# A graph attention layer on one core: the spread of the attention vectors and the order of the first group

## The chip, the cores and the metric

The kernel runs on one core of one Trainium2 chip. The metric is the time on the device in microseconds, from the first to the last instruction of the core; times of a kernel are the median of several executions. The kernel before took 2331.45 us (three executions, 2331.03 to 2332.3). Times inside the kernel are counted from the start of its span.

The engines are called TensorE (PE in the profile; its weight loads are PEld), VectorE (DVE), ScalarE (ACT), GpSimd (POOL) and SyncE (SP, which only issues transfers). Each works through its own queue in order and waits for the others by semaphores.

## The reference

`x` is 128 graphs of 64 nodes with 512 features, all fp32. Cut to what matters:

```python
h = relu(layernorm(x))                               # (128, 64, 512)
# layer 1: H = 4 heads, W_heads (4, 512, 512), a_heads (4, 1024)
Wh = einsum('bnf,hfo->bhno', h, W_heads)
f1 = einsum('bhno,ho->bhn', Wh, a_heads[:, :512])
f2 = einsum('bhno,ho->bhn', Wh, a_heads[:, 512:])
e  = f1[..., :, None] + f2[..., None, :]
e  = where(e > 0, e, 0.01 * e)
e  = where(adj > 0, e, -1e9)                         # one adj (64, 64) for all graphs
h1 = elu(softmax(e) @ Wh)                            # heads side by side: (128, 64, 2048)
# layer 2: the same with one head, W_out (2048, 512), a_out (1024)
out = elu(gat(h1, adj, W_out, a_out))
y   = relu(out @ w1 + b1) @ w2 + b2 + out            # w1, w2 (512, 512)
result = x + layernorm(y) * gamma + beta
```

## The kernel before

The 8192 rows are 64 tiles of 128 rows (two graphs each), and 16 groups of four tiles. The matrix products of most of the work are done by a fast scheme with 7 block products in place of 8. It needs sums of blocks of each weight matrix ("weight sums"), which GpSimd computes once, in the first group, and stores to DRAM (`tc`), from where they are loaded like weights. The first group (g = 0) is different from the others: it computes `h W` head by head with plain products (`head_w`), so that TensorE has work before the sums are there.

The scores need `W a` for each head. The two halves of `a` of head m are spread over 128 partitions by a product with a column of the identity (`spread_a`), and VectorE multiplies them with the rows of W and adds up (`fold`) into `wa`. `project_f` then multiplies `wa` with the transposed h.

```python
X[0] = load(0)
ar = wk.tile([2 * H, O], FP, tag="elu", name="ar", bufs=3)
nc.sync.dma_start(out=ar, in_=a_heads.rearrange("h (r p) -> (h r) p", p=O))
# ... cut: the other tiles of the group, adj, masks

mats = [W_heads[h] for h in range(H)]                          # matrices 0 to 3
mats += [W_out[h * O:(h + 1) * O, :] for h in range(H)]        # 4 to 7
mats += [w1, w2]                                               # M1 = 8, M2 = 9
homes = ("h11", "h22", "h12", "wh2", "out", "hS", "out", "hS", "out", "out")

def spread_a(m):
    ab = []
    for c in range(2):
        pb = flat(bank(f"pab{m}_{c}"))
        r = 2 * m + c
        nc.tensor.matmul(
            pb, ident[0:2 * H, r:r + 1].to_broadcast([2 * H, P]), ar, start=True, stop=True
        )
        ab.append(pb)
    return ab

def weight_sums(m, after=None):       # four tensor_tensor on GpSimd, then two stores to TC[m]
    ...

def norm1(t):
    # ... cut: bn_stats, bn_aggr, + eps on VectorE
    # rstd (pow) and nb = -mean * rstd on GpSimd
    LAST["nb"] = nc.gpsimd.tensor_scalar(nb, mean, rstd, -1.0, ALU.mult, ALU.mult)
    HN[t] = big.tile([P, F], FP, tag="hn", name=f"hn{t}", bufs=G)
    nc.scalar.activation(HN[t], X.pop(t), AF.Relu, bias=nb, scale=rstd)

def transpose_h(t):                   # 4 transposes on TensorE, a copy on ScalarE (pth, hT)
    ...

def project_f(g):
    # ... cut: 16 small products into pf
    L = sm.tile([P, 2, P], FP, tag="L", name=f"L{g}", bufs=1)
    for q in range(2):
        nc.scalar.activation(L[:, q], pf, AF.Identity, bias=isq[:, q, 1:2], scale=isq[:, q, 0:1])
    U = sm.tile([P, P], FP, tag="U", name=f"U{g}", bufs=1)
    nc.vector.tensor_scalar(U, pf, isf[:, 1:2], isf[:, 0:1], ALU.mult, ALU.add)
    R = sm.tile([P, H, P], FP, tag="R", name=f"R{g}", bufs=1)
    eng = nc.vector if g == 0 else nc.gpsimd
    eng.tensor_tensor(R, U[:, None, :].to_broadcast([P, H, P]),
                      headrow[:, :, None].to_broadcast([P, H, P]), ALU.mult)

def head_w(m, j):                     # h W of head m, tile j: four products, a copy on ScalarE
    pb = aux([P, O], f"hw{m}_{j}")
    for k in range(KC):
        LAST["pe"] = LAST["hw", m, j] = nc.tensor.matmul(
            pb, HT[j][:, k, :], MT[m][:, k, :], start=k == 0, stop=k == KC - 1)
    nc.scalar.copy(flat(HW[j][:, m]), pb)
```

`scores1` makes the scores of a group (s1pe), `attn_weights(p)` the softmax of two tiles (a chain of eight instructions on VectorE and one on ScalarE, ending in s1A), `transpose_weights(p)` turns them (s1pt, at). `attend0(h, r)` multiplies the weights with h W (pu) and applies elu, `turn0(h, r)` transposes the result (ptu) into h11, h12, hS, h22. `project2` is the product with W_out (g_b), `project1` of the groups from 1 on is the product with W_heads (g_a). The softmax of the second layer has the names s2.

The first group before, in the order in which it is written down (a scheduler moves some of it by its priorities):

```python
for t in range(G):
    norm1(t)
for t in range(G, 2 * G):
    prefetch(t)
norms, scores, turns = stage_a(1)
ab = [spread_a(m) for m in range(3)]
for m in range(3):
    fold(m, ab[m])
for j in range(G):
    transpose_h(j)
    head_w(0, j)
weight_sums(0, LAST["nb"])
fold(3, spread_a(3))
masks()
weight_sums(1, LAST["nb"])
for j in range(3):
    head_w(1, j)
more_sums(4)                # fetch and weight_sums
project_f(0)
weight_sums(2, LAST["nb"])
head_w(1, 3)
more_sums(5)
head_w(2, 0)
scores1(0)
attn_weights(0)
attn_weights(1)
weight_sums(3, LAST["nb"])
norms[0]()                  # norms of tiles 4 and 5
norms[1]()                  # 6 and 7
more_sums(6)
new_h1(0)
for j in range(1, G):
    head_w(2, j)
more_sums(7)
transpose_weights(0)
head_w(3, 0)
attend0(0, 0)
attend0(1, 0)
head_w(3, 1)
# ... cut: attends and turns of the four heads, the rest of head_w(3)
for g in range(NG):
    # ... cut
    if g == 0:              # project2(0) with this beside it, the sums of w1 and w2 last
        mixed = side1 + attn[:2] + norms[:1] + attn[2:] + norms[1:] + [nothing] * 3
        run(project2(g), mixed + early + scores + turns + [
            load_rows, lambda: sums_late(M1), lambda: sums_late(M2)
        ])
```

Of the kernel before, what the change touches and what calls it, by code (L numbers as in the profile page):

```python
# [22 lines left out]
def gat_preln_kernel(  # L23
# [87 lines left out]
    ar = wk.tile([2 * H, O], FP, tag="elu", name="ar", bufs=3)  # L111
    nc.sync.dma_start(out=ar, in_=a_heads.rearrange("h (r p) -> (h r) p", p=O))
# [11 lines left out]
    isq = const.tile([P, 2, 2], FP, name="isq")  # L124
    wa = const.tile([P, KC, 32], FP, name="wa")

    def masks():
# [8 lines left out]
        nc.vector.tensor_reduce(isf, id32[:, 0:2 * H].rearrange("p (c h) -> p c h", c=2), AX.X, ALU.add)  # L136
        for q in range(2):
# [17 lines left out]
    homes = ("h11", "h22", "h12", "wh2", "out", "hS", "out", "hS", "out", "out")  # L155
    MT, TC = {}, {}

    def fetch(m, after=None):
# [3 lines left out]
        if after is not None:  # L162
            behind(ins, after, "not in front of what is needed first")

    def spread_a(m):

        ab = []
        for c in range(2):
            pb = flat(bank(f"pab{m}_{c}"))
            r = 2 * m + c  # L170
            nc.tensor.matmul(
                pb, ident[0:2 * H, r:r + 1].to_broadcast([2 * H, P]), ar, start=True, stop=True
            )
            ab.append(pb)
# [12 lines left out]
    def weight_sums(m, after=None):  # L187
# [11 lines left out]
        nc.gpsimd.tensor_tensor(s[1][:, 1], b21, s[0][:, 1], ALU.subtract)  # L199
        TC[m] = [dram.tile([P, 2, 2, Q], FP, name=f"tc{m}_{i}") for i in range(2)]  # L200
        for i in range(2):
            nc.gpsimd.dma_start(out=TC[m][i], in_=s[i])

# [111 lines left out]
    def norm_stats(src, tag, t):  # L315
# [4 lines left out]
        if tag == "n1" and t >= G:  # L320
            behind(ins, LAST["pe"], "x may come late: not in front of what is urgent")
# [10 lines left out]
    def norm1(t):  # L332
# [6 lines left out]
        nc.scalar.activation(HN[t], X.pop(t), AF.Relu, bias=nb, scale=rstd)  # L339
# [8 lines left out]
    def transpose_h(t):  # L348
        pt = aux([P, KC, P], f"pth{t}")
        for k in range(KC):  # L350
            nc.tensor.transpose(pt[:, k, :], HN[t][:, ts(k, P)], ident)
        HT[t] = wk.tile([P, KC, P], FP, tag="hT", name=f"hT{t}", bufs=4)
        nc.scalar.copy(HT[t], pt)

    def project_f(g):
# [12 lines left out]
        for q in range(2):  # L368
            nc.scalar.activation(L[:, q], pf, AF.Identity, bias=isq[:, q, 1:2], scale=isq[:, q, 0:1])
        U = sm.tile([P, P], FP, tag="U", name=f"U{g}", bufs=1)  # L370
        nc.vector.tensor_scalar(U, pf, isf[:, 1:2], isf[:, 0:1], ALU.mult, ALU.add)
        R = sm.tile([P, H, P], FP, tag="R", name=f"R{g}", bufs=1)
        eng = nc.vector if g == 0 else nc.gpsimd
        eng.tensor_tensor(
            R, U[:, None, :].to_broadcast([P, H, P]), headrow[:, :, None].to_broadcast([P, H, P]),
            ALU.mult,
        )
# [460 lines left out]
    for t in range(G):  # L838
# [5 lines left out]
    ab = [spread_a(m) for m in range(3)]  # L844
    for m in range(3):
        fold(m, ab[m])
    for j in range(G):
        transpose_h(j)
        head_w(0, j)
# [142 lines left out]
```

## Time and profile before

| engine | busy us | instructions |
|---|---|---|
| TensorE, products | 2289.5 | 11856 |
| TensorE, weight loads | 1896.2 | 11856 |
| VectorE | 1274.2 | 2227 |
| ScalarE | 901.9 | 1621 |
| GpSimd | 1014.9 | 908 |

The span of the profiled execution is 2329.7 us. The mean granted clock of TensorE over it was 0.995 of full speed.

The page of a profile has the busy time of each engine, then the span in 40 equal slices in which a digit is the busy share of a slice in tenths. Other views of the same trace are the timeline (each line: start, duration, engine, line of the kernel, operation, output<-input, sizes, count, and in brackets the idle time before it and what ended it), and the list of waits (who waited for what: total, times, longest).

A busy TensorE in this trace is not always a fast one: the duration of one pass has to be looked at beside the share. In the first group the page cannot show much, since a slice of it is 58 us long; the timeline from 0 to 230 us is the view that the change is read from.

### The profile page before, as it was taken

To read this page: it belongs to the slowest core of one execution; us is meant where nothing else is said; L and a number is where in the kernel's file an instruction comes from. 1 tells how busy PE (TensorE), PEld (TensorE's weight loads), DVE (VectorE), ACT (ScalarE), POOL (GpSimd) and SP (SyncE) were. 2 spreads that over 40 slices of the span, in tenths; PEclk is the share of its full clock that TensorE was granted. 3 is DMA by queue.
4 is the path that set the end of the run, shared out by engine and by line. 5 is a ranking of instruction groups with operands and counts; after the bars stand their busy time and mean duration, and the time that the engine had idled before them with its cause. 6 is when DMAs were issued, how large, how long until landed. Compare 5 with 4: busy or idle time off the path is not lost. (4 is left out here: it accounts for less than half of the span.)

```text
span 2329.7 us, 33260 instructions
## 1 busy us (share of the span) xinstructions
PE 2289.5 (98%) x11856; PEld 1896.2 (81%) x11856; DVE 1274.2 (55%) x2227; ACT 901.9 (39%) x1621; POOL 1014.9 (44%) x908
## 2 busy tenths in 40 slices
PE   8899999999999999999999999999999999999997
PEld 3477888888888888888888888888888888888885
DVE  4645464554656555464654655556465554644527
ACT  2523525244252533525244252533525344251512
POOL 6554443525444253443524444263443535433334
PEclk9999999999999999999999999999999999999999
DMA  7435454454545545454454645445454454635543
GB/s 271 163 109 176 132 181 131 147 175 132 183 134 159 158 136 181 135 177 131 146 180 128 185 136 159 156 136 183 132 171 137 146 180 132 181 122 161 165 149 104
DMA packets 255011, 361.14 MB, mean 155 GB/s; under 512 B 23768, under 2 KB 143608, under 8 KB 254848
## 3 DMA queue, kind: packets, MB, share of 16 engines
q1 hardware_dynamic: 249744, 341.16, 47.1%
q0 software_dynamic: 4576, 16.81, 2.0%
q8 instruction: 96, 1.57, 0.3%
q10 hardware_dynamic: 528, 1.05, 0.1%
q14 instruction: 67, 0.55, 0.1%
HBM read 331.66 MB, written 27.26 MB: 154 GB/s over the span
## 5 line engine op out<-in xcount | busy, mean ns | idle before, releaser
L297 PE MATMUL g_b<-w,h 128*128 128x256 f32 x2560 | 593.1, 379 | 0.0
L297 PEld LDWEIGHTS g_b<-w,h 128*128 128x128 f32 x2560 | 481.1, 190 | 64.7 <-issue 2.1
L282 PE MATMUL g_a<-z,w 128*128 128x256 f32 x1440 | 342.8, 381 | 0.0
L282 PE MATMUL g_a<-zs_z,w 128*128 128x256 f32 x1440 | 338.0, 383 | 4.0 <-ACT t_a L248 4.0
L282 PEld LDWEIGHTS g_a<-zs_z,w 128*128 128x128 f32 x1440 | 271.0, 191 | 64.0 <-issue 24.3
L282 PEld LDWEIGHTS g_a<-z,w 128*128 128x128 f32 x1440 | 273.3, 191 | 41.8 <-DVE g_a L586 4.9
L297 PE MATMUL g_b<-w,hS 128*128 128x256 f32 x1024 | 239.3, 380 | 0.0
L590 POOL TENSOR_TENSOR hS<-hS,h 128x512 f32<-128x512 f32 x60 | 77.9, 1299 | 354.3 <-DVE hS L556 354.3
L297 PEld LDWEIGHTS g_b<-w,hS 128*128 128x128 f32 x1024 | 192.7, 191 | 25.1 <-issue 0.2
L554 ACT ACTIVATE exc<-g_a 128x512 f32<-128x512 f32 x240 | 142.7, 594 | 163.4 <-DVE g_a L586 95.6
L556 DVE SCALAR_TENSOR_TENSOR h<-exc,g_a 128x512 f32<-128x512 f32 x180 | 123.6, 686 | 141.9 <-ACT exc L555 141.3
L555 ACT ACTIVATE exc<-exc 128x512 f32<-128x512 f32 x240 | 151.4, 631 | 6.7
L671 POOL TENSOR_TENSOR h<-h,h 128x512 f32<-128x512 f32 x64 | 86.9, 1366 | 132.9 <-PE g_b L297 132.9
L671 POOL TENSOR_TENSOR h<-hS,h 128x512 f32<-128x512 f32 x64 | 81.3, 1272 | 144.0 <-PE g_b L297 144.0
L472 ACT COPY at<-s1pt 128x512 f32<-128x512 f32 x64 | 34.6, 590 | 280.7 <-PE s1pt L468 280.7
L307 POOL TENSOR_TENSOR zs_z<-zS,z 128x512 f32<-128x512 f32 x60 | 84.6, 1410 | 130.6 <-PE g_a L282 121.2
L813 POOL TENSOR_TENSOR xr<-xr,bs 128x512 f32<-128x512 f32 x64 | 94.3, 1477 | 73.3 <-DMA xr<-in_x_dram 39.7
L297 PE MATMUL g_d<-w,rt 128*128 128x256 f32 x512 | 121.8, 380 | 2.1 <-DVE o L805 1.0
L282 PE MATMUL g_c<-ot,w 128*128 128x256 f32 x512 | 122.8, 383 | 0.6 <-DVE ot L775 0.6
L695 DVE SCALAR_TENSOR_TENSOR jf<-wh,ao 128x512 f32<-128x512 f32 x128 | 98.0, 801 | 33.0 <-ACT wh L677 32.9
L282 PE MATMUL g_a<-zS,w 128*128 128x256 f32 x480 | 113.4, 379 | 0.0
L297 PEld LDWEIGHTS g_d<-w,rt 128*128 128x128 f32 x512 | 96.9, 190 | 17.2 <-DVE o L805 2.3
(162 smaller groups left out, 3538.6 us busy)
## 6 DMA issues: line engine op xcount, KB each, us to landing
w<-tc SPq DMA_DIRECT2D x624, 256.0 KB, 2.7
w<-in_L_gnn_W_out_dram SPq DMA_DIRECT2D x192, 256.0 KB, 2.7
w<-in_L_gnn_W_heads_dram SPq DMA_DIRECT2D x180, 256.0 KB, 3.1
w<-in_L_gnn_w_dram SPq DMA_DIRECT2D x96, 256.0 KB, 2.7
x<-in_x_dram SPq DMA_DIRECT2D x64, 256.0 KB, 4.1
xr<-in_x_dram SPq DMA_DIRECT2D x128, 128.0 KB, 2.6
out_dram<-o SPq DMA_DIRECT2D x128, 128.0 KB, 2.4
tc<-pt POOLq DMA_DIRECT2D x20, 512.0 KB, 3.8
```

The lines of the kernel that those rows point to most:

```text
L282: LAST["pe"] = nc.tensor.matmul(bk[:, o, :], w[:, k, ts(o, P)], a[:, k, :], start=start and o == 0 and k == 0, stop=k == 1, skip_group_che ...
L297: LAST["pe"] = nc.tensor.matmul(bk[:, j, :], a[:, k, ts(j, P)], w[:, k, :], start=start and k == 0 and j == 0, stop=i == len(ms) - 1 and k ...
L307: eng.tensor_tensor(s2, s1, a11, ALU.subtract)
L472: nc.scalar.copy(AT[t].rearrange("p b h n -> p (b h) n"), pt)
L554: nc.scalar.activation(ex, src, AF.Relu, scale=-1.0)
L555: nc.scalar.activation(ex, ex, AF.Exp, scale=-1.0)
L556: nc.vector.scalar_tensor_tensor(dst, ex, -1.0, src, ALU.add, ALU.max)
L590: nc.gpsimd.tensor_tensor(dst, dst, H1["22"][:, h], ALU.add)
L671: nc.gpsimd.tensor_tensor(dst[:, h], x0[:, h], x1[:, h], ALU.subtract)
L695: nc.vector.scalar_tensor_tensor(junk, WH2[g][:, j], 1.0, ao[:, c, :], ALU.mult, ALU.mult, accum_out=f[:, c, j:j + 1],)
L813: nc.gpsimd.tensor_tensor(xr, xr, bs, ALU.add)
```

## The change

The change is to the first group alone. It has these parts:

- The spread of `a` uses all 128 rows of the array: `ar` is a full tile whose other rows are set to zero, and the column of the identity has 128 rows. The spreads of heads 1 to 3 come one by one between the transposes and the `h W` of head 0, with explicit dependencies that keep them in place, where six of the eight products stood at the start before.
- The factor R of groups 0 and 1 is made by four instructions on ScalarE straight from the projection (with `hsf`, two more small instructions of the masks), in place of U and R on VectorE or GpSimd.
- The norms of tiles 4 to 7 depend on the last fold (VectorE) and on an `h W` (ScalarE), and the sums of matrix 2 stand before them on GpSimd and the sums of matrix 3 behind them.
- The fetches and sums of matrices 4 to 7 have a fixed order, matrix 6 goes to another buffer, and the sums of w1 and w2 are moved from the end of the first `project2` into the `h W` of head 3 and the beginning of `project2`.
- Attends and turns of head h are put one after the other between the `h W` of heads 2 and 3, with the transposes of the next group's tiles among them; those of the last heads go beside the first products of `project2`.

```diff
-    ar = wk.tile([2 * H, O], FP, tag="elu", name="ar", bufs=3)
-    nc.sync.dma_start(out=ar, in_=a_heads.rearrange("h (r p) -> (h r) p", p=O))
+    ar = wk.tile([P, O], FP, tag="elu", name="ar", bufs=3)
+    nc.vector.memset(ar, 0.0)
+    nc.sync.dma_start(out=ar[0:2 * H], in_=a_heads.rearrange("h (r p) -> (h r) p", p=O))
...
-    homes = ("h11", "h22", "h12", "wh2", "out", "hS", "out", "hS", "out", "out")
+    homes = ("h11", "h22", "h12", "wh2", "out", "hS", "h22", "out", "out", "out")
...
-            nc.tensor.matmul(
-                pb, ident[0:2 * H, r:r + 1].to_broadcast([2 * H, P]), ar, start=True, stop=True
-            )
+            ins = nc.tensor.matmul(pb, ident[:, r:r + 1].to_broadcast([P, P]), ar, start=True, stop=True)
+            if after is not None:
+                behind(ins, after, "not in front of it")
...
         if tag == "n1" and t >= G:
-            behind(ins, LAST["pe"], "x may come late: not in front of what is urgent")
+            behind(ins, LAST["pe" if t >= 2 * G else "fold"], "not in front of what is urgent")
...
-        nc.scalar.activation(HN[t], X.pop(t), AF.Relu, bias=nb, scale=rstd)
+        ins = nc.scalar.activation(HN[t], X.pop(t), AF.Relu, bias=nb, scale=rstd)
+        if t == 1:
+            behind(ins, LAST["hT"], "the first product waits for it")
+        if G <= t < 2 * G:
+            behind(ins, LAST["pe"], "not in front of what is urgent")
...
+        if g < 2:
+            for h in range(H):
+                nc.scalar.activation(
+                    R[:, h], pf, AF.Identity, bias=hsf[:, 0, h:h + 1], scale=hsf[:, 1, h:h + 1]
+                )
...
-    ab = [spread_a(m) for m in range(3)]
-    for m in range(3):
-        fold(m, ab[m])
-    for j in range(G):
-        transpose_h(j)
-        head_w(0, j)
+    fold(0, ab)                          # ab = spread_a(0), ahead of transpose_h(0)
+    fold(1, spread_a(1, LAST["th"]))
     weight_sums(0, LAST["nb"])
-    fold(3, spread_a(3))
+    head_w(0, 0)
+    transpose_h(1)
+    fold(2, spread_a(2, LAST["pe"]))
+    head_w(0, 1)
+    transpose_h(2)
+    fold(3, spread_a(3, LAST["pe"]))
+    weight_sums(1, LAST["nb"])
+    weight_sums(2, LAST["nb"])
+    head_w(0, 2)
+    transpose_h(3)
+    head_w(0, 3)
     masks()
...
+    head_w(1, 0)
     project_f(0)
+    head_w(1, 1)
+    norms[0]()
+    norms[1]()
+    weight_sums(3, LAST["nb"])
+    sums_of(4, LAST["hw", 0, 0])         # fetch and weight_sums
     scores1(0)
     attn_weights(0)
     attn_weights(1)
+    head_w(1, 2)
+    head_w(1, 3)
+    fetch(5, LAST["hw", 0, 2])
+    fetch(6, LAST["hw", 1, 3])
+    ahead = fetch(7, LAST["hw", 1, 3])
+    ahead = weight_sums(5, ahead)
+    head_w(2, 0)
+    ahead = weight_sums(6, ahead)
+    head_w(2, 1)
+    transpose_weights(0)
+    weight_sums(7, ahead)
+    new_h1(0)
+    head_w(2, 2)
+    transpose_weights(1)
+    attend0(0, 0)
+    head_w(2, 3)
+    attend0(1, 0)
+    turn0(0, 0)
     head_w(3, 0)
+    attend0(2, 0)
+    turn0(1, 0)
+    transpose_h(4)
     head_w(3, 1)
...
+    head_w(3, 3)
+    sums_of(M1, LAST["hw", 3, 0])
     attend0(1, 1)
+    turn0(3, 0)
+    transpose_h(7)
+    side1 = [
+        lambda: (attend0(2, 1), turn0(1, 1)), lambda: (attend0(3, 1), turn0(2, 1), project_f(1)),
+        lambda: turn0(3, 1), lambda: (scores1(1), attn_weights(2)), nothing, lambda: attn_weights(3),
+        lambda: (fetch(M2, LAST["hw", 3, 3]), weight_sums(M2, LAST["pe"])), nothing,
+    ] + turns[1:] + [nothing] * 2
...
-            run(project2(g), mixed + early + scores + turns + [
-                load_rows, lambda: sums_late(M1), lambda: sums_late(M2)
-            ])
+            run(project2(g), mixed + early + scores + turns + [load_rows])
```

## The prediction

> **What bounds the kernel now.** I read the page's busy shares first:
>
> ```profile
> PE 2289.5 (98%) x11856; PEld 1896.2 (81%) x11856; DVE 1274.2 (55%) x2227; ACT 901.9 (39%) x1621; POOL 1014.9 (44%) x908
> ...
> PEld 3477888888888888888888888888888888888885
> ```
>
> TensorE is busy for 98% of the span. The second line is its weight loads in 40 slices of 58 us: 8 tenths everywhere except in the first four slices (3, 4, 7, 7) and the last. So what is left to gain lies in the first 230 us, the first group, which is the part that the change rewrites. The waits of TensorE, for all 2329.7 us, say the same:
>
> ```profile
> PE hw L612 <- ACT hw L615: 7.5, 1, 7.5
> PE pab L171 <- POOL n1rs L327: 5.4, 1, 5.4
> PE g_a L282 <- ACT t_a L248: 4.0, 1, 4.0
> PE pth L351 <- ACT hT L353: 3.2, 2, 2.6
> PE s1pt L468 <- DVE s1A L426: 2.6, 2, 2.1
> ```
>
> All five waits fall before 215 us. A busy TensorE can also be a slow one, so the timeline of TensorE comes next (start, duration, what, count of passes; the four products of an h W are eight passes):
>
> ```profile
> 5.36 10.57 PE L171 MATMUL pab<-ar,ident 8*128 8x512 f32 x12 [5.36 <-POOL n1rs L327]
> 15.87 1.11 PE L351 MATMUL pth<-ident,hn 128*128 128x128 f32 x4
> 16.91 2.07 PE L171 MATMUL pab<-ar,ident 8*128 8x512 f32 x2
> 18.91 5.46 PE L612 MATMUL hw<-pw,hT 128*128 128x512 f32 x8
> ...
> 25.78 3.70 PE L612 MATMUL hw<-pw,hT 128*128 128x512 f32 x8
> ...
> 58.54 7.13 PE L612 MATMUL hw<-pw,hT 128*128 128x512 f32 x16
> 73.21 5.61 PE L612 MATMUL hw<-pw,hT 128*128 128x512 f32 x8 [7.53 <-ACT hw L615]
> ...
> 214.72 3.78 PE L282 MATMUL g_a<-zs_z,w 128*128 128x256 f32 x8 [4.05 <-ACT t_a L248]
> ```
>
> Three losses are to be seen. (1) The spreads of eight rows take 10.57/12 = 0.88 us a pass, and the first h W takes 5.46 us where the next one takes 3.70: half speed from 5.36 to about 22.5 us, though TensorE never stops. (2) It stands still for 7.53 us at 65.7, and starts again slowly (5.61). (3) It stands still for 4.05 us at 210.7, with 3.78 for 1.89 after it.
>
> Behind (2) stand ScalarE and GpSimd. ScalarE's queue is in order, and the norm of the next group stands in it ahead of the eviction of an h W; its factor comes from GpSimd, which is in the weight sums until 66.2:
>
> ```profile
> 57.62 0.59 ACT L615 COPY hw<-hw 128x512 f32<-128x512 f32 x1 [2.85 <-PE hw L612]
> 68.81 1.52 ACT L339 ACTIVATE hn<-x,n1nb,n1rs 128x512 f32<-128x512 f32 x2 [10.60 <-POOL n1nb L337]
> ```
>
> Behind (3) stands one VectorE instruction. In the first group it takes 5.48 us, in the second 0.42:
>
> ```profile
> 207.96 5.48 DVE L418 SCALAR_TENSOR_TENSOR s2e<-s2e 128x256 f32<-128x256 f32 x1
> ...
> 354.50 0.42 DVE L418 SCALAR_TENSOR_TENSOR s2e<-s2e 128x256 f32<-128x256 f32 x1
> ```
>
> GpSimd worked without a gap from 202.08 to 214.57 meanwhile: the weight sums of w2, then the sums of z that had queued behind them.
>
> **What the Trainium skill says.** "TensorE: Matmul & The Clock Gate", Part 1, What's actually happening: the array idles at half clock, and some 3.4 us of sustained work release it. The trace agrees in part: from the first h W at 18.91 the weight loads shorten from 0.33 to 0.19 us at 22.49, after 3.6 us. But 10.57 us of work on eight rows did not release it; the page doesn't say that the count of rows matters, so I take that from the trace. "SBUF — State Buffer", Who interferes with whom: a VectorE instruction with two SBUF inputs contends with a GpSimd instruction that reads SBUF, and one fully blocks. The 5.48 against 0.42 us agrees; the folds (one input in PSUM) agree too, at 0.68 us each beside GpSimd at work.
>
> **The change, part by part.** I replay the new order of TensorE with the steps of the trace. Start to start: an h W 3.43 us (its evictions at 39.25, 42.68, 46.12 and 49.55 us), a spread pair 1.72 warm and 3.42 cold, four transposes of h 0.53, a projection 1.0, a score step 1.02, a pair of transposed weights 0.9, an attend or a turn of head 0 to 3 1.0.
>
> Start. The memset of the full `ar` stands ahead of its load. A 128x128 memset took 0.17 us, four times the width should stay under 0.5; the load's issue moves from 1.17 to about 1.3 us. TensorE starts at about 5.45.
>
> Spread and h W of head 0. 5.45 + 3.42 (first pair, cold) + 1.0 (transposes) = 9.9; by then 4.4 us of full-row work have passed, so the clock is up: + 1.72 + 3.43 = 15.1 for the first h W. Then 0.53 + 1.72 + 3.43 twice gives 26.4. The spread also covers the copy of the transposed h, which cost 0.73 us each at 29.9 and 34.8. The last tile has no spread: 0.5 + 0.75 wait + 3.43 = 31.1. VectorE's folds take 32 x 0.61 us from 10.65, as before, to 30.1, and are in nobody's way.
>
> To the first product of the second layer. h W of head 1 tile 0 (34.5), projection (35.5), tile 1 (39.0), scores (40.0; the factors L and R now come from ScalarE, 2 x 0.4 + 4 x 0.4 us, ready at about 38.1 in place of a 2.94 us R on VectorE), two more h W (46.8), two of head 2 (53.7), weights (54.6), h W (58.0), weights (58.9), attend and h W (63.4), attend and turn (65.4). Then four rounds: h W 3.43 + attend 1.0 + turn 1.0 + transposes 0.5 = 5.9 each, so 89.0. What still has to be done and was done before the first g_b in the old order: two attends, three turns, one projection, 6.0 us. That makes 95.0, against 115.1 in the trace: 20.1 us less. By cause: about 6.6 the clock, 0.7 a wait, 9.4 the stall at 65.7 (7.53 + 1.9 slow), the remaining 3.4 small waits of 101 to 110 us, where attends and turns of one head followed too closely.
>
> The stall must not come back. The sums of matrix 2 now stand before the norms of tiles 4 to 7: GpSimd ends the sums of 0 and 1 at 24.5 as before, and matrix 2 (4 x 1.23 + 1.1 + two issues of a fetch 1.6) at 32 to 36, as its buffers' stores land. The factors take some 4.3 us more, ready at 37 to 41. ScalarE does the four h (4 x 0.76) behind the h W that ends at 39.0, by 42.2 to 43.5; the next eviction that TensorE depends on is wanted at 46.8. So 3 us of slack.
>
> Stall at 210. The sums of w1 and w2 move from there into the h W of head 3 and the first products of the second layer. The stretch from the first g_a to the transposed weights of the second softmax (s2pt) takes 224.54 - 189.35 = 35.19 us in the first group and 364.92 - 336.86 = 28.06 in the second. Without those sums the first should equal the second: 7.1 us less.
>
> What it adds. Those sums now lie beside the softmax of tiles 4 to 7, whose three-step chain on VectorE has two SBUF inputs in three of eight instructions. In the old order two of these were stretched by 1.1 and 0.7 us and TensorE waited 2.1. I put 2.5 us on more of it. The wait at 159.6 (2.6 us and 1.9 slow; a norm behind six sums of z on GpSimd) keeps its order and stays.
>
> Sum: 20.1 + 7.1 - 2.5 = 24.7 us less. All later groups have the same order on TensorE, VectorE, ScalarE and GpSimd. 2331.45 - 24.7 = 2306.8.
>
> **The rivals.** First: the full-row spread doesn't raise the clock, since 120 of its rows are zeros and the array may count arithmetic, not rows. For it: only eight-row spreads were seen. Then the second pair, its neighbours and half of the first h W stay slow, and the gain shrinks by some 3.5 us: 2310. Second: a new wait takes the place of the old one. TensorE now changes between h W, attend, turn and transposes every microsecond, with ScalarE in order between them; a round gives ScalarE 3.6 us and VectorE 2.7 us of work in 5.9, so it fits, but one late link costs each of four rounds. And GpSimd is, by this replay, nearly without a pause from 12 to 117 us in the new order; if the softmax of tiles 4 to 7 is blocked as L418 was, 5 us come back, and a stop of over 3 us costs 2 more at half clock: 2313 to 2316. Third: the gain is larger, because attends, turns and first g_b interleaved cover the softmax that cost 2.1 us, and the wait at 159.6 goes too: 2300. Fourth: only the first group gains nothing because weights arrive late. Against it: the DMA engines are full until 30 us in both, and TensorE never waited for a weight there.
>
> **Range and chances.** The centre is 2307. A second stall costs up to 10 us, the third rival gives 7: low 2299, high 2318. The gain that would be over 2%, 46.6 us, exceeds all idle and slow time that I find in the first 230 us (about 24 us of waits with the 5.4 of the start, and some 15 at half speed), and nothing in the order could cost 46. So nearly all lies within 2%.
>
> **What will show it.** Passes of the second spread pair at 0.43 us and not 0.88; the first h W at 3.7 us, ending near 15; no wait of TensorE for the eviction of h W; the first attend near 59 and the last turn near 98; L418 of the first group at about 0.4 us; g_a to s2pt in about 28 us. If the wait for s1A grows above 3 us, or a wait for a turn's or attend's copy shows up in each round, the second rival holds. If the end of the first group is early by 20 us but the total is not, a later group has changed, and I am wrong about that.

## The result, and the profile after

The changed kernel takes 2320.09 us (median of four executions, 2317.49 to 2322.69), the kernel before, measured with it, 2331.53 us. The ratio is 0.9951 [0.9933, 0.9968]: a gain of 11 us, under half of the 24.7 predicted, and 2 us outside the range. The profiled executions have spans of 2318.7 and 2329.7 us, the same 11.0 us apart, so the two traces can be compared piece by piece.

The page already shows that one slice went the wrong way (busy us, share and instructions; then the weight loads in 40 slices of 58 us):

```profile
PE 2279.3 (98%) x11856; PEld 1893.2 (82%) x11856; DVE 1288.4 (56%) x2227; ACT 903.3 (39%) x1629; POOL 1017.0 (44%) x907
...
PEld 4568888888888888888888888888888888888885
```

TensorE is busy for 10 us less, and the first two slices went from 3 and 4 to 4 and 5. But the third fell from 7 to 6 (its granted clock from 0.97 to 0.87), which no step of the prediction foresaw. VectorE's busy time grew by 14.2 us with the same count of instructions. The list of TensorE's waits names the place (total, times, longest):

```profile
PE s1pt L485 <- DVE s1A L443: 14.3, 2, 14.1
PE pab L177 <- DMA ar<-in_L_gnn_a_heads_dram: 6.6, 1, 6.6
PE pth L362 <- ACT hT L364: 2.4, 1, 2.4
```

The waits for the eviction of an h W (7.5) and for t_a (4.0) are gone. The wait for s1A, the last step of the softmax of tiles 4 and 5, has grown from 2.6 to 14.3 us.

The timeline of TensorE (start, duration, output<-input, count of passes, and in brackets the wait ahead), at the start, around that wait, and from there to the second softmax:

```profile
6.58 3.75 PE L177 MATMUL pab<-ar,ident 128*128 128x512 f32 x4 [6.58 <-DMA ar<-in_L_gnn_a_heads_dram]
10.12 1.06 PE L362 MATMUL pth<-ident,hn 128*128 128x128 f32 x4
10.97 2.30 PE L177 MATMUL pab<-ar,ident 128*128 128x512 f32 x4
13.11 3.60 PE L629 MATMUL hw<-pw,hT 128*128 128x512 f32 x8
...
100.82 1.04 PE L662 MATMUL ptu<-ident,nat 128*128 128x128 f32 x8
...
106.37 3.62 PE L304 MATMUL g_b<-w,hS 128*128 128x256 f32 x16
124.06 1.94 PE L485 MATMUL s1pt<-ident,s1A 128*128 128x128 f32 x8 [14.08 <-DVE s1A L443]
...
184.20 1.46 PE L289 MATMUL g_a<-z,w 128*128 128x256 f32 x6
...
213.62 0.60 PE L740 MATMUL s2pt<-ident,s2A 128*128 128x128 f32 x4
```

The clock is up within the second spread pair, and the first h W runs at full speed. At 110 us TensorE stops for 14.08 us, then starts at half clock (1.94 us, where the other half of these transposes takes 1.04).

On VectorE it is one instruction, the leak of the scores (L435, `max(0.01 e, e)`), with both inputs in SBUF. For tiles 0 and 1 it takes 0.69 us, for tiles 4 and 5 it takes 14.76:

```profile
42.61 0.69 DVE L435 SCALAR_TENSOR_TENSOR s1e<-s1e 128x512 f32<-128x512 f32 x1
...
105.36 14.76 DVE L435 SCALAR_TENSOR_TENSOR s1e<-s1e 128x512 f32<-128x512 f32 x1
120.16 0.69 DVE L436 TENSOR_REDUCE s1mx<-s1e 128x8 f32<-128x512 f32 x1
```

And on GpSimd, at the beginning and the end of that stretch (L672 and L688 are sums for the first product of the second layer, L205 a sum of w2, L208 its stores):

```profile
103.66 1.28 POOL L688 TENSOR_TENSOR h<-hS,h 128x512 f32<-128x512 f32 x1
104.89 2.50 POOL L672 TENSOR_TENSOR hS<-hS,h 128x512 f32<-128x512 f32 x2
...
118.32 1.25 POOL L205 TENSOR_TENSOR pt<-pw,pt 128x512 f32<-128x512 f32 x1
119.53 1.10 POOL L208 DMA_DIRECT2D tc<-pt  x2
```

From 103.66 to 119.57 us GpSimd runs thirteen sums of 1.25 us, each starting 0.03 to 0.06 us before the one in front ends. The leak ends 0.55 us after the last of them, a little less than its normal 0.69 us.

**The account.** The changed kernel has as much done 98.2 us after the start as the old one after 115.1 (the last turn, from 100.82, is through at 101.7; less two g_b of 1.73 that were already done by then): 16.9 gained. The stretch from the first g_a to the transposed weights of the second softmax is 213.62 - 184.20 = 29.42 us, of which 1.26 is a pair of s1 transposes that lay elsewhere before, so 28.16 where it was 35.19: 7.0 gained. 16.9 + 7.0 = 23.9, and 11.0 came out, so some 12.9 us are lost between. The waits for s1A grew by 11.7, and slow products follow the long one, so the stop accounts for the loss within about a microsecond.

### The profile page after: what moved, and what is told of

Same layout as the page of the kernel before. It is cut to its first block, busy times and chain, and to the rows that moved or that the text cites. A ratio compares the mean times of both kernels' runs of the same rounds, so it can differ in the third digit from the quotient of the medians.

```text
span 2318.7 us, 33251 instructions
## 1 busy us (share of the span) xinstructions
PE 2279.3 (98%) x11856; PEld 1893.2 (82%) x11856; DVE 1288.4 (56%) x2227; ACT 903.3 (39%) x1629; POOL 1017.0 (44%) x907
## 5 line engine op out<-in xcount | busy, mean ns | idle before, releaser
L688 POOL TENSOR_TENSOR h<-h,h 128x512 f32<-128x512 f32 x64 | 86.8, 1364 | 135.1 <-PE g_b L304 135.1
L688 POOL TENSOR_TENSOR h<-hS,h 128x512 f32<-128x512 f32 x64 | 81.1, 1268 | 142.6 <-PE g_b L304 142.6
```

What stands on the lines that cost most here:

```text
L688: nc.gpsimd.tensor_tensor(dst[:, h], x0[:, h], x1[:, h], ALU.subtract)
```

## The experiments

The texts on record call the theories by letters. **A**: the leak and its like are held by GpSimd's reads of SBUF, and let go when GpSimd stops; this is what the second rival of the prediction names. **C** came after the first four runs: an instruction of GpSimd that is ready behind the running one goes first, and only a wait for its direct predecessor lets VectorE in. The later letters, and the rivals, are told in the texts themselves. Where there is one execution, its time alone shows little under 5 us (the four of the changed kernel lie from 2317.49 to 2322.69); smaller differences are read from the trace.

**Scores in PSUM.** The chain for tiles 4 to 7 stays in PSUM, so that no step but the last has two inputs in SBUF. The leak becomes a scaled copy on ScalarE and a maximum on VectorE.

```diff
+                if t in (2, 3):
+                    es, ei = ei, pe[:, i:i + n]
...
-            nc.vector.scalar_tensor_tensor(ei, ei, ALPHA, ei, ALU.mult, ALU.max)
+            if f1 is None and t in (2, 3):
+                nc.scalar.activation(es, ei, AF.Copy, scale=ALPHA)
+                nc.vector.tensor_tensor(ei, ei, es, ALU.max)
```

> The changed kernel, with the softmax of tiles 4 to 7 kept in PSUM: no VectorE instruction of that chain but the last small copy has both inputs in SBUF (the leak is a copy on ScalarE times 0.01 and a maximum on VectorE). GpSimd's work stays as it is. Theory A (the leak instruction of 14.76 us was held off by GpSimd because it has two SBUF inputs): every instruction of the chain takes 0.7 to 0.8 us, TensorE's wait for s1A falls from 14.1 us to under 3, and the kernel gains 11 to 14 us, to 2306 to 2309. Theory B (VectorE as a whole, or the scores, are held up by something else that lasts until 120 us, such as a load or a store of sums): one instruction of the chain still lasts until about 120 us and the time stays at 2320.

Measured: 2313.1 us, ratio to before 0.9919 [0.9903, 0.9936]. The leak takes 0.70 us now, but the last step of the chain, a small copy from SBUF to SBUF, is held in its place (timeline of VectorE):

```profile
105.85 0.70 DVE L439 TENSOR_TENSOR s1pe<-s1pe,s1e 128x512 f32<-128x512 f32 x1
...
111.86 10.75 DVE L454 COPY s1A<-s1A 128x128 f32<-128x128 f32 x1
```

So only 7 us came back, and the copy is one more instruction that can be held. That a copy can be held agrees with "SBUF — State Buffer", Who interferes with whom, of the Trainium skill, which counts copies among the operations that can take the shared pair of ports.

**Sums of w2 behind the softmax**, which shortens GpSimd's uninterrupted stretch.

```diff
-        lambda: (fetch(M2, LAST["hw", 3, 3]), weight_sums(M2, LAST["pe"])), nothing,
+        lambda: (fetch(M2, LAST["hw", 3, 3]), weight_sums(M2, LAST["A"])), nothing,
```

> The changed kernel, with only the weight sums of w2 made to wait for the end of the softmax of tiles 6 and 7. Theory A (the leak instruction gets through when GpSimd first stops): GpSimd runs from about 103.7 us through ten adds and subtractions to about 114.7 and then has nothing to do until TensorE has done the next product, so the leak instruction takes 9.3 us instead of 14.76, TensorE's wait falls from 14.1 to about 8.6 us, and the kernel gains 5 to 6 us. Theory A2 (one GpSimd instruction blocks it once, and the rest is another cause): no change to the 14.76 us.

Measured: 2314.15 us (one execution). GpSimd stops at 115.14, and the leak ends 0.55 us later, as in the changed kernel:

```profile
104.15 11.54 DVE L435 SCALAR_TENSOR_TENSOR s1e<-s1e 128x512 f32<-128x512 f32 x1
...
112.67 2.47 POOL L688 TENSOR_TENSOR hS<-h,h 128x512 f32<-128x512 f32 x2
```

The end is where A puts it. The duration came out 2.2 us longer than expected: the leak began 1.2 us earlier, GpSimd stopped 0.4 us later, and the leak ends 0.55 us behind the stop. What is fixed is the moment of release.

**More reads** (eight more additions on GpSimd beside the softmax, all into one tile, of no use to the result):

```diff
+    def more():
+        d = big.tile([P, 2, Q], FP, tag="rt1", name="dmy")
+        for _ in range(8):
+            nc.gpsimd.tensor_tensor(d, H1["22"][:, 0], H1["12"][:, 0], ALU.add)
```

> The changed kernel, with eight more GpSimd additions of 128x512 (results not used) put among the sums of the first group, 8 x 1.25 = 10 us of work that reads SBUF. Theory A: the stretch in which GpSimd does not stop grows by 10 us, the leak instruction takes 24 to 25 us instead of 14.76, and the kernel is 10 us slower. Theory B: the leak instruction keeps its 14.8 us, and the time changes by less than 4 us.

Measured: 2315.39 us (one execution). A clear miss: with more work on GpSimd the leak was *not* held (VectorE, then GpSimd).

```profile
104.43 1.06 DVE L435 SCALAR_TENSOR_TENSOR s1e<-s1e 128x512 f32<-128x512 f32 x1
...
100.96 5.66 POOL L933 TENSOR_TENSOR dmy<-h,h 128x512 f32<-128x512 f32 x4
```

TensorE waited 9.0 us for GpSimd's late sums of hS instead. The new additions write one tile, so each has a wait for the one in front. This gave theory C.

**More memsets** (eight memsets of 128x512 on GpSimd behind the first subtractions; `wait_for` is `behind`, which adds a dependency):

```diff
+                    last = nc.gpsimd.tensor_tensor(dst[:, h], x0[:, h], x1[:, h], ALU.subtract)
+                if g == 0 and what == "s1":
+                    d = big.tile([P, 2, Q], FP, tag="ot1", name="dmy")
+                    for _ in range(8):
+                        wait_for(nc.gpsimd.memset(d, 0.0), last, "beside the softmax")
```

> The changed kernel, with eight more GpSimd memsets of 128x512 (results not used) behind the last subtraction of the first block row; three of them stand in a row in the middle of the busy stretch, at about 112 us. They only write SBUF. Theory A in its narrow form (only GpSimd's reading of SBUF holds off a two-input instruction): the leak instruction ends at about 112 us, after 7 us in place of 14.76, and the kernel gains 5 to 8 us although GpSimd has more to do. Theory A in its wide form (any GpSimd instruction holds it off): it ends when GpSimd first stops, later than 120 us, and the kernel is 2 to 5 us slower.

Measured: 2317.05 us (one execution). The leak ends at 113.34, 0.55 us after the last subtraction (112.79), and the first memset begins at 112.85. That fits two readings, that a memset doesn't read and that the first memset waits for the subtraction directly in front of it, so it decides nothing.

**Nothing of the chain in SBUF alone.** As the first run, and the small copy is replaced by a product that reads PSUM.

```diff
-                LAST["A"] = nc.vector.tensor_copy(A[:, u, H], A[:, u, 0])
+                if t in (2, 3):
+                    LAST["A"] = nc.vector.tensor_tensor(
+                        A[:, u, H], ei.rearrange("p (t h) m -> p t h m", h=H)[:, :, 0],
+                        ri.rearrange("p (t h) -> p t h", h=H)[:, :, 0:1].to_broadcast([P, n // H, N]), ALU.mult)
```

> As the kernel with the softmax of tiles 4 to 7 in PSUM, and the small copy that ended its chain (SBUF to SBUF, held off for 10.75 us there) made a small product of a PSUM and an SBUF operand. No VectorE instruction of the chain has two inputs in SBUF, and none copies from SBUF to SBUF. GpSimd's work is that of the changed kernel. Theory A: no instruction of the chain takes over 1 us, TensorE's wait for s1A falls to under 2 us, 2305 to 2309 us. Theory B (the last step of the chain is always held up until GpSimd stops, whatever its operands): a wait of about 10 us stays, 2313 us.

Measured: 2304.26 us (2303.94 to 2304.67), ratio 0.9883 [0.9866, 0.9899]: 15.8 us under the changed kernel. No instruction of the chain is held, beside a GpSimd that works as before:

```profile
106.12 0.70 DVE L439 TENSOR_TENSOR s1pe<-s1pe,s1e 128x512 f32<-128x512 f32 x1
...
111.53 0.28 DVE L455 TENSOR_TENSOR s1A<-s1pe,s1r 128x128 f32<-128x128 f32 x1
```

So it is shown what is held, the steps with two inputs in SBUF and the small copy, and what that costs. That it is GpSimd's reading which holds them, and none of its other work, is not separated by any run. The wait for s1A is 0.2 us.

**Waits on GpSimd.** The changed kernel with its work unchanged, but the sums of this stretch on GpSimd wait for the ones in front (core of the edit):

```diff
+            if h:
+                behind(add, LAST["add"], "one after the other")
...
+                    if g == 0 and h:
+                        wait_for(sub, LAST["sub"], "one after the other")
```

> The changed kernel with GpSimd's instructions in the same work, but each add of hS behind the add before it, each subtraction behind the one before it, and the four sums of w2 one behind the other, so that at about 106, 111 and three times from 114 us an instruction waits for the very one in front of it. The order of TensorE is unchanged. Theory C (a two-input VectorE instruction gets in only where GpSimd stops between two instructions, and a wait on the instruction in front is such a stop, however short; where the next one is ready it never gets in): the leak instruction ends at about 107 us, after 2 to 3 us in place of 14.76, later ones of the chain wait for the next such place, TensorE's wait falls from 14.1 to 5 to 9 us, the kernel gains 5 to 9 us. Theory D (VectorE is held off as long as GpSimd has work, and the eight additions that let it through were different for another reason): the leak instruction lasts until about 120 us as before, 2320 us.

Measured: 2306.74 us (one execution). The leak takes its normal time, and the waits for s1A sum to 2.7 us:

```profile
104.76 0.69 DVE L441 SCALAR_TENSOR_TENSOR s1e<-s1e 128x512 f32<-128x512 f32 x1
```

13 us came from waits alone, more than expected. C predicts the sign; the next runs show that its mechanism is not the right one.

**One wait.** Only the addition of head 2 waits for that of head 1.

```diff
+            if h == 2:
+                behind(add, LAST["add"], "one after the other")
+            LAST["add"] = add
```

> The changed kernel with one wait more: on GpSimd the addition of head 2 of hS waits for that of head 1, its direct predecessor, near 106 us; nothing else is changed. Theory C (an instruction that is ready behind the running one takes over before VectorE can; a wait for the predecessor opens a gap): the leak, 14.76 us in the changed kernel, gets in at that gap and ends near 107 us, 2 to 3 us long, and the next instruction of the chain with two inputs in SBUF is held instead, until GpSimd stops near 120 us; TensorE's wait for s1A stays between 8 and 14 us. Theory D (one gap does nothing; the additions that waited everywhere helped because they slowed GpSimd as a whole): the leak takes 14 to 15 us as before.

Measured: 2307.88 us (one execution). Neither C nor D holds as put. VectorE got in at the one wait, and at the later boundaries too, where no wait was added (timeline of VectorE, then of GpSimd):

```profile
105.40 0.83 DVE L435 SCALAR_TENSOR_TENSOR s1e<-s1e 128x512 f32<-128x512 f32 x1
...
112.66 1.06 DVE L435 SCALAR_TENSOR_TENSOR s1e<-s1e 128x512 f32<-128x512 f32 x1
```

```profile
111.90 1.27 POOL L691 TENSOR_TENSOR h<-hS,h 128x512 f32<-128x512 f32 x1
113.13 1.72 POOL L691 TENSOR_TENSOR hS<-h,h 128x512 f32<-128x512 f32 x1
```

The second leak begins at 112.66, is held until GpSimd's sum ends at 113.17, and runs then; the next sum, begun at 113.13, takes 1.72 in place of 1.27, so now it is the one that waits. In the changed kernel the same kind of boundary let VectorE in at none of eleven.

**The wait earlier**, before VectorE wants anything: the addition of head 1 waits for the subtraction in front of it.

```diff
+                    if g == 0 and h == 0 and what == "s1":
+                        wait_for(LAST["add", 1], sub, "one after the other")
```

> The changed kernel with one wait more on GpSimd, like the run with one wait (2307.9 us), but one addition earlier: the addition of head 1 of hS waits for its direct predecessor, the subtraction of head 0, near 104.9 us, some 0.4 us before the leak of tiles 4 and 5 is due; behind it GpSimd has no wait for a direct predecessor until 118 us. Reading G (VectorE has to be waiting when GpSimd leaves a gap; once it has got in it gets its turn again, and a gap that comes too early does nothing): the leak is held for 12 to 15 us as in the changed kernel, and the total is 2317 to 2321 us. Reading H (a wait changes how GpSimd's later instructions follow one another, whoever waits at that moment): the leak takes under 2.5 us, the chain goes on, and the total is 2306 to 2310 us.

Measured: 2307.15 us (one execution). Reading H holds (GpSimd, then VectorE):

```profile
104.87 1.27 POOL L674 TENSOR_TENSOR hS<-hS,h 128x512 f32<-128x512 f32 x1
106.09 1.73 POOL L674 TENSOR_TENSOR hS<-hS,h 128x512 f32<-128x512 f32 x1
```

```profile
105.73 0.95 DVE L437 SCALAR_TENSOR_TENSOR s1e<-s1e 128x512 f32<-128x512 f32 x1
```

The gap of the wait (104.79 to 104.87 us) is over when the leak comes, and the leak still gets its turn at the next boundary, in front of the sum begun at 106.09. A gap at the right moment is not what it takes: theory C falls. The wait changes how GpSimd's later instructions follow one another. What, then, had set GpSimd to keep VectorE out? In both old and new kernel a transfer had been issued by GpSimd just before.

**No issue.** The changed kernel with no dependency added among its sums, but the two stores of the sums of w1 and the fetch of w2 come behind the softmax, so that GpSimd issues nothing between the last sum of w1 (which waits for its direct predecessor) and the contention.

```diff
-            nc.gpsimd.dma_start(out=TC[m][i], in_=s[i])
+            LAST["tc", m, i] = nc.gpsimd.dma_start(out=TC[m][i], in_=s[i])
...
-        lambda: (fetch(M2, LAST["hw", 3, 3]), weight_sums(M2, LAST["pe"])), nothing,
+        lambda: (
+            [behind(LAST["tc", M1, i], LAST["A"], "no issue before it") for i in range(2)],
+            fetch(M2, LAST["A"]), weight_sums(M2, LAST["pe"]),
+        ), nothing,
```

> The changed kernel with no transfer issued by GpSimd between the last sum of w1 (near 99.3 us, which waits for its direct predecessor) and the end of the softmax of tiles 4 to 7: the two stores of the sums of w1 and the fetch of w2 come behind that softmax. GpSimd still runs its additions and subtractions of hS and h without a stop from about 102 to 113 us, and no wait is added among them. Reading I (after a transfer is issued GpSimd's instructions follow one another so that VectorE is kept out, and after a wait for the direct predecessor they let it in until the next issue): the leak takes under 2 us, and TensorE's wait for s1A is under 4 us. Rival J (issues have nothing to do with it; only a wait among these additions helps): the leak is held until GpSimd stops, 6 to 10 us, and the wait for s1A is 6 to 10 us.

Measured: 2309.78 us (one execution), wait for s1A 2.7 us in all, and a new wait of 2.8 us for zS (VectorE, then GpSimd):

```profile
104.92 1.21 DVE L435 SCALAR_TENSOR_TENSOR s1e<-s1e 128x512 f32<-128x512 f32 x1
```

```profile
101.74 1.26 POOL L672 TENSOR_TENSOR hS<-hS,h 128x512 f32<-128x512 f32 x1
103.08 1.27 POOL L688 TENSOR_TENSOR h<-hS,h 128x512 f32<-128x512 f32 x1
104.31 1.27 POOL L672 TENSOR_TENSOR hS<-hS,h 128x512 f32<-128x512 f32 x1
105.54 1.72 POOL L672 TENSOR_TENSOR hS<-hS,h 128x512 f32<-128x512 f32 x1
```

That is what reading I asks for, but the run has a wait that its expectation did not count on. In the changed kernel the fetch (102.86) stands between the addition of head 0 of hS and the subtraction that reads it. Without the fetch the subtraction (L688) stands directly behind that addition and waits for it, with a gap like the one in the run before (here 103.00 to 103.08 us). So this run cannot tell the absence of issues from that wait.

**Issue behind the wait.** The kernel with the earlier wait, and the fetch of w2 put directly behind the addition that waits.

```diff
-        lambda: (fetch(M2, LAST["hw", 3, 3]), weight_sums(M2, LAST["pe"])), nothing,
+        lambda: (wait_for(fetch(M2, LAST["hw", 3, 3]), LAST["add", 1], "behind it"), weight_sums(M2, LAST["pe"])), nothing,
```

> The kernel of the run before this call (2307.15 us: the addition of head 1 of hS waits for its direct predecessor), with the fetch of w2 on GpSimd moved from 102.7 us to directly behind that addition, near 106 us. Reading I (an issue brings back the state in which VectorE is kept out): the leak gets in during the issue, and a later instruction of the chain with two inputs in SBUF is held for 6 us or more, until GpSimd stops or waits for its direct predecessor near 118 us; TensorE's wait for s1A is 6 us or more and the total 2312 us or more. Rival J: no instruction of the chain takes over 2 us, and the total is 2306 to 2309 us.

Measured: 2320.83 us (one execution), wait for s1A 13.2 us. The leak gets in at the pause of 0.30 us ahead of the issue, and the instruction after the next is held for 13.68 us (GpSimd, then VectorE):

```profile
105.92 0.78 POOL L168 DMA_DIRECT2D pw<-in_L_gnn_w_dram  x1 [0.30 <-POOL hS L674]
106.72 1.28 POOL L674 TENSOR_TENSOR hS<-hS,h 128x512 f32<-128x512 f32 x1
```

```profile
105.62 0.69 DVE L437 SCALAR_TENSOR_TENSOR s1e<-s1e 128x512 f32<-128x512 f32 x1
106.35 0.69 DVE L438 TENSOR_REDUCE s1mx<-s1e 128x8 f32<-128x512 f32 x1
107.07 13.68 DVE L439 TENSOR_TENSOR s1e<-s1e,s1mx 128x512 f32<-128x512 f32 x1
```

So one half of reading I is tested, by this run and the one with the earlier wait: behind a wait for the direct predecessor VectorE got in at boundary after boundary, and one issue behind that wait locked it out again, in one execution each. The other half, that without an issue VectorE would get in with no wait at all, is not shown. The traces agree with both halves. In the kernel before, GpSimd issues its stores at 207.10, L418 is held from the next sum (208.22) on, and it ends at 213.44, where one sum waits for its direct predecessor (a gap from 213.15 to 213.23). And in the changed kernel GpSimd issues nothing after 120.6 us, and in the later groups, though GpSimd's sums and pauses go on, none of 26 leaks takes over 1.06 us (shortest, median and longest, in ns):

```profile
L435 DVE SCALAR_TENSOR_TENSOR s1e<-s1e x26: 692/877/1061, 285.2 to 1981.3; 128x512 f32<-128x512 f32 x26
```

What in GpSimd keeps this apart is open; no run looks inside.

**Eight rows.** The changed kernel with the old spread of eight rows, without the memset.

```diff
-    ar = wk.tile([P, O], FP, tag="elu", name="ar", bufs=3)
-    nc.vector.memset(ar, 0.0)
+    ar = wk.tile([2 * H, O], FP, tag="elu", name="ar", bufs=3)
...
-            ins = nc.tensor.matmul(pb, ident[:, r:r + 1].to_broadcast([P, P]), ar, start=True, stop=True)
+            ins = nc.tensor.matmul(pb, ident[0:2 * H, r:r + 1].to_broadcast([2 * H, P]), ar, start=True, stop=True)
```

> The changed kernel with the spread of eight rows again (no memset, the load of a as before), in the new order. Theory A (eight-row products don't raise the clock): the array stays slow until 3.6 us into the first h W: second pair at 0.88 us a pass (3.5 us in place of 2.14), first h W about 5.3 us in place of 3.43; but a comes 1 us earlier. First h W ends at about 18 us in place of 16.5, the kernel is 1 to 3 us slower. Theory B (the clock comes up by time of work, whatever the rows): first h W ends at about 15.5, the kernel is 1 us faster.

Measured: 2323.29 us (one execution), 3.2 us above the median of the changed kernel and 0.6 above its slowest execution. It starts 1.1 us earlier, and the clock is still down when the first h W begins (5.35 us, where it takes 3.60 in the changed kernel):

```profile
5.46 3.75 PE L176 MATMUL pab<-ar,ident 8*128 8x512 f32 x4 [5.46 <-POOL n1rs L333]
9.14 1.12 PE L361 MATMUL pth<-ident,hn 128*128 128x128 f32 x4
10.19 3.78 PE L176 MATMUL pab<-ar,ident 8*128 8x512 f32 x4
13.89 5.35 PE L628 MATMUL hw<-pw,hT 128*128 128x512 f32 x8
```

So rows of zeros do count. "TensorE: Matmul & The Clock Gate", Part 1, What's actually happening, of the Trainium skill, speaks of sustained work and not of rows; here the rows made the difference. The total doesn't measure the spread alone, though: the waits for s1A differ too (13.2 us in place of 14.3).

**Warm first.** Nine products of the identity with itself while TensorE waits for `a`: once with the changed kernel, once with the kernel in PSUM.

```diff
+    warm = flat(bank("warm"))
+    for i in range(9):
+        nc.tensor.matmul(warm[:, 0:P], ident, ident, start=True, stop=True)
```

> The changed kernel with nine products of the identity with itself (128x128, result not used) ahead of the first spread, in the time in which TensorE waits for a. Theory A (about 3.6 to 5 us of work on all rows raise the clock, whatever is computed): TensorE starts at 2.5 us, the first pair takes about 1.8 to 2.4 us in place of 3.54, transposes 0.5, the second pair 1.75, and the first h W starts at 10.6 to 11.2 us in place of 13.1. The kernel gains 2 us. Theory B (zeros and ones don't raise it): no change in the pairs, first h W at 13.1 us.

> The kernel with the softmax of tiles 4 to 7 in PSUM throughout (2304.26 us), plus nine products of the identity with itself (18 passes) on TensorE while it waits for the attention vectors. With the changed kernel these products brought the first h W forward by 1.55 us and the total not at all; my reading was that the wait for s1A, which ended when GpSimd stopped, took the gain up. Here that wait is gone. If the reading is right: about 1.5 us less than 2304.3, 2302.8 us. Rival: the early microseconds are taken up anyway by another link of the first group, such as the folds of VectorE or the order of GpSimd's sums: 2304.3 us, and another wait of TensorE before 100 us grows by 1.5 us.

Measured: 2320.97 us (one execution) with the changed kernel, no gain, though the first h W started 1.55 us earlier (11.56 us in place of 13.11): the long wait for s1A grew from 14.1 to 15.4 us, because GpSimd sets the moment of release. In PSUM: 2302.82 us (2301.13 to 2303.17), ratio 0.9879 [0.9864, 0.9893], by its medians 1.4 us under the kernel without them. That agrees with the expectation but does not show it: the kernel before was 1.6 us faster in that measurement too (2329.99 against 2331.62). The start, in PSUM:

```profile
2.48 4.21 PE L869 MATMUL warm<-ident 128*128 128x128 f32 x18 [2.48 <-POOL ident masks.py:199]
6.48 2.64 PE L177 MATMUL pab<-ar,ident 128*128 128x512 f32 x4
...
9.39 1.88 PE L177 MATMUL pab<-ar,ident 128*128 128x512 f32 x4
11.11 3.60 PE L640 MATMUL hw<-pw,hT 128*128 128x512 f32 x8
```

The first h W starts 2.1 us before that of the kernel in PSUM without them (13.23), and it is still 2.1 us ahead when TensorE has waited for a copy of the transposed h, near 145 us (first line without them, second with them):

```profile
146.42 1.15 PE L362 MATMUL pth<-ident,hn 128*128 128x128 f32 x8 [2.40 <-ACT hT L364]
144.31 1.80 PE L362 MATMUL pth<-ident,hn 128*128 128x128 f32 x8 [2.40 <-ACT hT L364]
```

But there the kernel with them starts slowly, and the next products take it 2.90 us in place of 1.89. At the first g_a 0.5 us of the lead is left (166.50 against 166.99).

**Norms before the sums of z**, on top of that, for the wait near 160 us that the prediction let stand (`zs` marks the sums of z just begun, `nb1` is the factor of the norm of tile 11):

```diff
+        if LAST.get("zs") in ((1, 0), (1, 1)) and "nb1" in LAST:
+            behind(ins, LAST["nb1"], "the norms come first")
```

> The same, and the norms of tiles 8 to 11 before two of the sums of z on GpSimd, so that ScalarE's h of these tiles, and behind it the copy of the transposed h, come sooner. This is for the wait of 2.4 us for that copy near 160 us, which the prediction let stand together with 1.9 us of slow products after it. If the norm is what that copy waits for: the wait falls under 0.5 us and the total to about 2299 us (2302.8 less 3.5 to 4). Rival: the sums of z are themselves wanted by then; TensorE waits for z instead, about 2 us, and the total stays at 2302 to 2304 us.

Measured: **2298.66 us** (2298.23 to 2299.57), ratio 0.9863 [0.9847, 0.9879], the fastest of all, 21 us under the changed kernel. The wait for the copy of the transposed h, 2.4 us in the changed kernel and in the one this was built on, is gone from the list. The two longest that are left are 2.5 us, for the identity at the start, and 1.1 us.

## Why the prediction was wrong, step by step

**The start (5.45 us): wrong by 1.1.** The memset took 0.48 us, as estimated, but the load behind it was issued at 1.41 and not 1.3, and TensorE began 5.17 us after the issue, where it had been 4.19 us before (1.17 to 5.36). The profile names GpSimd's n1rs for the start before, but the spread reads only `ar` and the identity, and the identity was written by 2.43 us, so there too it was the load. Why the load took 1 us longer is not shown. Without the memset the start is 5.46.

**Spread and h W of head 0: right, but for half a pair.** The clock came up within the second spread pair (2.30 us, predicted 1.72) and not before it; the first h W ended at 16.5 in place of 15.1, of which 1.1 is the start. The first rival (zeros don't count) falls with the run of eight rows.

**To the first product of the second layer: right in its mechanism, 3.2 us short.** No wait for the eviction of an h W is left, the first attend came at 60.9 (59), and the equal point at 98.2 (95.0): 16.9 of 20.1 us.

**The stall at 210: right.** 7.0 us of 7.1; L418's successor took 0.42 us.

**The wait at 159.6: right that it stays.** 2.39 us and 1.97 for the slow transposes.

**What it adds (2.5 us): this step failed.** It measured about 12.9, almost all of it one wait of 14.1 us for s1A and the slow products behind it. The mechanism stands in the text, there and in the second rival, and the runs in PSUM show it. Its size was off by a factor of five. "I put 2.5 us on more of it" took two stretched instructions of the old order as a measure, and the rival took the 5.48 us of L418. Neither is a property of the instruction. The two (118.78 and 123.57 us) lay behind a pause of GpSimd of 5.19 us that ended at 114.92, with no transfer issued since 91.69, and each was stretched past one boundary at most. L418 was held over four sums and let go at a wait: the prediction read GpSimd's run from 202.08 to 214.57 as one without a gap, but the trace has gaps of 0.08 us in it, one of them at 213.15. The prediction also counted three of eight instructions that can be held, and the small copy is a fourth.

"SBUF — State Buffer", SBUF: two separate sides, of the Trainium skill says that whichever starts first, a VectorE instruction with two SBUF inputs or a GpSimd instruction, has the shared pair of ports "for the whole instruction", and the other fully blocks. Taken by itself that would bound a block at one GpSimd instruction, 1.25 us. Here VectorE was kept out over a dozen of them, and the measurement decides: the length of the block was the rest of GpSimd's uninterrupted run. My replay had the number for it. It says that GpSimd "is, by this replay, nearly without a pause from 12 to 117 us" and puts the softmax of tiles 4 to 7 at its end. To ask when GpSimd would next stop, rather than how long such a block had been elsewhere, gives 117 less the 105 at which the leak came, 12 us, where 14.8 were measured.

With that step put right, the measured pieces add up. 2331.5 less 16.9, 7.0 and the old wait of 2.6 is 2305.0, and the kernel whose chain stays in PSUM measured 2304.3.

The gain was thus not hidden by something that would have bounded the kernel anyway: the sums that were moved away from 210 us, where they had cost 7, stood at 105 us in the way of another chain, where they and the sums of hS cost 13.

## What to carry to other kernels

Before work is moved onto GpSimd, list what VectorE does beside it with two inputs in SBUF or as a copy from SBUF to SBUF, and where GpSimd has issued a transfer before its run of sums, count a block until GpSimd's next stop or wait for its direct predecessor, not one instruction. Where such a chain is on the path, keep one input of each of its steps in PSUM (15.8 us here), or give GpSimd one wait for its direct predecessor behind the last transfer that it issues (12 to 13 us here). And ask of a gain made ahead of a stop whether the stop moves with it: 1.55 us of earlier work were worth nothing here, since the end of the stop stayed where GpSimd put it.

## What was not expected of the hardware

- One VectorE instruction of 0.69 us took 14.76 us beside GpSimd sums of 1.25 us, a copy of 128x128 took 10.75 us, and one wait on GpSimd brought the leak to 0.83 to 0.95 us, later ones to 1.06.
- Whether GpSimd lets VectorE in between two of its instructions depends on what GpSimd did before: held after it issued a transfer (14.76, 11.54 and 13.68 us), let in after a wait for its direct predecessor (0.69 to 1.26 us in the four runs with such waits and no issue behind them, while GpSimd's own sums grew from 1.27 to 1.72 us). One pair of runs, of one execution each, tests the issue directly (2307.15 and 2320.83 us); whether VectorE gets in without any wait where no transfer was issued, and why all this is so, is open.
- Products of eight rows leave the clock down (3.78 us for the second pair, and 5.35 for the h W behind it); the same products with 120 rows of zeros had it up 6.5 us after the start (3.60 for that h W).
